# A routed transformer block on one core: the end of the router, the one-hot table products, the second layer's modulation and the W_down blocks rearranged

## The chip, the cores and the metric

The kernel runs on one core of a Trainium2 chip. The metric is device time in microseconds for one execution; a lower number is better. A core has a matrix engine (TensorE; the profile lists it as PE, and its weight loads as PEld), a vector engine (VectorE, DVE), an activation engine (ScalarE, ACT), a general engine (GpSimd, POOL) and a queue engine that issues transfers (SyncE, SP). They run side by side and wait for one another by semaphores. SBUF is the on-chip memory of 128 partitions, PSUM the memory that TensorE writes to, and everything larger lies in the chip's main memory.

## The reference, cut to what matters

Two transformer layers over 2048 tokens of width 512. Each layer is modulated by six vectors, made from a small vector c. Layer 0 has windowed attention and a mixture of 64 experts of which each token uses 8; layer 1 has attention and a gated feed-forward network with Hadamard transforms.

```python
mod = (_silu(L0_c) @ L0_wmod).reshape(1, 6, 1, -1)      # sa, ca, ga, sb, cb, gb
...
# router and experts of layer 0, x is (2048, 512)
probs = softmax(x @ gate_weight.T)                       # 64 experts
top_val, top_idx = lax.top_k(probs, 8)
top_val = top_val / top_val.sum(-1, keepdims=True)
mapping = ...                     # a secondary expert may be replaced by the most similar primary one
rerouted = mapping[top_idx]; rerouted[:, :4] = top_idx[:, :4]
order = argsort(rerouted.reshape(-1)); tok = order // 8
gate, up = split(ragged_dot(x[tok], gate_up_proj, group_sizes))
y = ragged_dot(silu(gate) * up, down_proj, group_sizes)
out = zeros_like(x).at[tok].add(y * w[:, None])
...
mod = (_silu(L1_c) @ L1_wmod).reshape(1, 6, 1, -1)       # layer 1's six vectors
...
# layer 1's feed-forward
x = fwht(x * SU_ug) / 64
x = silu((x @ W_gate.T) * s_gate) * ((x @ W_up.T) * s_up)
x = fwht(x * SU_dp) / 64
x = (x @ W_down.T) * s_dp
```

## The kernel before, in words

The 2048 tokens are 16 blocks of 128 (NT = 16, P = 128), kept in SBUF as x_sb. All matrix products are in 32-bit floats except the counting and one-hot ones, which are in 16-bit floats. A scheduler orders the instructions of each engine by their dependencies and the order of the program; `tc.issue_after` and the helper `in_turn` (L729) pin the order of some TensorE work to the order of the program.

**Attention of layer 0.** Half blocks are taken in turn; after every fourth block `route` (L432) sets two later steps. `logits` normalizes four blocks (xn_f), stores them in the main-memory table h_d, transposes them (nT_f) into hTr and multiplies by the gate weights (lg). `choose` takes the softmax, the best eight of each token (top), marks the chosen experts (sel) and transposes marks and shares (selT by st, pT by spT). While the attention runs, SP fills five sum tables in main memory (sums, NSUM = 5) with zeros; the source is the first slot of xring, a ring of NX = 12 slots of 128 x 576 numbers that later holds gathered token blocks.

**The router's end** (from L541). Counts of the choices (cnt), the map of replaced experts (map2), positions of each token in its expert's list (pf, and mT, the marks), the counts per expert (nq), a rank by size and its permutation (perm). `order` then gives SP the experts to fetch: `fetch_w` (L526) issues three transfers per expert, for the first four at once; the pool holds four experts' weights. Then the shares are brought into the order of ranks (pw, from mapT and mapr) and stored in h_d (L637); room, base, over, ot and the small products ops_ give the shift for lists longer than the room reserved for them, and jump and vT (L671 to L674) give each token's place in the table. vT is transposed (tv, L677) and copied to vm, and the eight largest entries per token (MAX8, L683) are split into a row, paf, and a column, tlf, of a table of 164 columns (ST = 164).

The table is written by one-hot products: for each block, hr marks the row (L692, then scaled by the token's number on ScalarE, L693) and hc the column (L695), each for all eight choices with the choice as the innermost index, and 128 products in all add up in tps:

```python
hr = rh.tile([P, P, TOPK], F16, tag="hr", name=f"hr_{i}")
V.tensor_tensor(hr, iota8[:, 0:P, :], bc(paf[:, i, :], 1, P), ALU.is_equal)
S.activation(hr, hr, AF.Copy, scale=con("tok1")[:, i : i + 1])
hc = rh.tile([P, ST, TOPK], F16, tag="hc", name=f"hc_{i}")
V.tensor_tensor(hc, iota8[:, 0:ST, :], bc(tlf[:, i, :], 1, ST), ALU.is_equal)
for k in range(TOPK):
    mm(tps, hr[:, :, k], hc[:, :, k], n == 0, n == NT * TOPK - 1)
```

From tps come hole and tidx (L701, L702), the table of token numbers from which GpSimd gathers. Small steps for lists that overflow follow (le, eps_, of, rps), and then `modulate` (L180) makes layer 1's six vectors: for each a 1 MB weight tile wm (two at a time), and either 16 products of one column (the four "col" vectors) or four products 512 wide (the two "gate" vectors). The matrix products all go through the helper on L129.

**The experts** (loop of L912). 64 runs of the table are taken in 32 pairs q. A run has up to ROOM[q] places (440 in the first pair, 184 in the last), in blocks of 128. `fetch_x` (L733) gathers a run's blocks from h_d into xring (L522), `x_T` transposes them (xp, L749) and modulates them (xT, L752 and L754), `gate_up` makes gu for both runs and gub for the two rests together, `down` makes y, scales it (yo, L804) and `add_rows` scatters it into the sum tables (L808). Pair 0's blocks are all transposed before its first product. Later pairs' transposes are spread between the products by `take`.

**Beside the experts**, VectorE and TensorE work on W_down: `gates` prepares small vectors, then `wd_step` (L848) takes eight blocks of 64 columns, each with four butterfly stages (L859, L860), two Hadamard products (wdh) and a store (L870) into wd_d. In the last quarter of the loop, `earlier` (L825) loads finished sum tables, in the memory of the W_down blocks, and adds them to x_sb.

**Layer 1** follows: attention, then the feed-forward loop that reads W_down back from wd_d as wd and multiplies four blocks by it (`down1`, L1264).

## Time and profile before

| | |
|---|---|
| time, median of 3 runs | 2269.71 us (2265.64 to 2273.39) |
| the profiled execution's own time | 2273.46 us |
| its span, first to last instruction | 2271.2 us |
| mean granted TensorE clock | 0.946 |
| busy share: PE, PEld, DVE, ACT, POOL | 93%, 51%, 37%, 21%, 25% |
| moved by DMA | 256.41 MB in 137350 packets, 52648 of them under 512 B |
| attention ends, cnt complete | about 331.6 us |
| tidx complete | 413.1 us |
| first expert product gu | 444.92 us |
| expert loop's last yo | about 1136 us |

How to read it: times inside the execution are microseconds from the start of the span. In a row of a group, the number after x is the count, then the total busy time and the mean in ns, and then the idle time in front of it with what ended it. A 32-bit matrix product shows as two records. The records of matrix products overlap, so the distance between two starts, not the length of one, is what a product costs in a row of them. The granted clock is 1.00 at full speed and 0.50 at half.

### The profile page before, as it was taken

Reading aid. Unit: us, or ns where it says so; the run is one execution under the profiler, and the core shown is the slowest. Engines: PE = TensorE matmul, PEld = TensorE weight load, DVE = VectorE, ACT = ScalarE, POOL = GpSimd, SP = SyncE. Lnnn points to the kernel's source line nnn. Section 1 sums busy time; section 2 is a strip of 40 time slices with the busy share of each in tenths; the row PEclk is TensorE's granted clock in tenths of the full one; section 3 lists DMA queues with packets and bytes.
Section 4 is the critical chain, followed back from the end, with each engine's and each line's share of the span. In section 5 each row is a group of like instructions: output and inputs, shape, how many; then the busy total and the mean of one; then the engine's idle time right before and its main releaser. Section 6 shows DMA issues by size and latency. Waiting matters only on the chain.

```text
span 2271.2 us, 27760 instructions
## 1 busy us (share of the span) xinstructions
PE 2103.9 (93%) x10584; PEld 1167.8 (51%) x10584; DVE 845.0 (37%) x2179; ACT 479.6 (21%) x1121; POOL 571.4 (25%) x448
## 2 busy tenths in 40 slices
PE   4899978899999999999809999998999999999999
PEld 3665555545555556666504555555444444444444
DVE  3236655154455433335547366765001011000101
ACT  0123423111111111111101166764010010010000
POOL 2300000366556666656424300110100010010000
PEclk9899975699999999999959989999999999999999
DMA  9800113569999989999862100003200000000000
GB/s 355 307 2 19 38 56 103 178 155 225 240 231 220 228 221 246 248 288 327 221 193 71 27 11 2 2 2 123 100 1 19 0 0 19 0 0 0 19 0 19
DMA packets 137350, 256.41 MB, mean 113 GB/s; under 512 B 52648, under 2 KB 55656, under 8 KB 134656
## 3 DMA queue, kind: packets, MB, share of 16 engines
q1 hardware_dynamic: 95136, 159.48, 21.1%
q0 software_dynamic: 36032, 77.30, 16.4%
q10 hardware_dynamic: 6048, 17.83, 2.1%
q8 instruction: 85, 1.39, 0.2%
q14 instruction: 49, 0.40, 0.1%
HBM read 180.56 MB, written 71.65 MB: 111 GB/s over the span
## 4 chain that ended last, share of the span: by engine, by line
PE 84%; DVE 6%; DMA 5%; ACT 3%; issue 1%; POOL 1%; ACTq 0%; POOLq 0%; DVEq 0%
PE y L129 19%; PE gu L129 10%; PE gate L129 10%; PE up L129 10%; PE gub L129 5%; PE s L129 4%; PE xp L749 4%; PE q L129 3%; PE po L129 3%; PE mod L129 3%; ACT pr L1123 2%; PE po_a L129 2%; PE pt L1141 2%; PE tps L129 2%; DMA wm<-in_L_wmod 2%; DMA sum<-yo,tidx 1%
## 5 line engine op out<-in xcount | busy, mean ns | idle before, releaser
L808 POOL DMA_INDIRECT sum<-yo,tidx x164 | 270.2, 1648 | 116.0 <-DMA sum<-yo,tidx 39.3
L522 POOL DMA_INDIRECT xring<-h_d,tidx x164 | 169.8, 1035 | 515.0 <-DVE tidx L702 331.4
L1280 DVE SCALAR_TENSOR_TENSOR act<-up,L_ws_up,sg 128x512 f32<-128x512 f32 x64 | 48.1, 751 | 587.0 <-PE up L129 587.0
L129 PE MATMUL gu<-xT,w 128*128 128x312 f32 (+26 forms) x1024 | 244.8, 397 | 5.4 <-DVE xT L754 5.4
L129 PE MATMUL gate<-xh,wug 128*128 128x512 f32 x512 | 232.3, 596 | 2.0 <-DMA wug<-in_L_Wug 2.0
L129 PE MATMUL up<-xh,wug 128*128 128x512 f32 x512 | 230.5, 592 | 0.0
L129 PE MATMUL y<-wd,act 128*128 128x512 f32 x512 | 229.5, 592 | 0.0
L129 PEld LDWEIGHTS gu<-xT,w 128*128 128x128 f32 x1024 | 191.4, 191 | 59.3 <-issue 16.7
L1278 ACT ACTIVATE sg<-gate,L_ws_gate 128x512 f32<-128x512 f32 x64 | 44.0, 687 | 570.1 <-PE gate L129 570.1
L129 PEld LDWEIGHTS gate<-xh,wug 128*128 128x128 f32 x512 | 97.4, 191 | 122.9 <-issue 120.7
L129 PEld LDWEIGHTS up<-xh,wug 128*128 128x128 f32 x512 | 97.3, 190 | 122.7 <-issue 122.5
L129 PEld LDWEIGHTS y<-wd,act 128*128 128x128 f32 x512 | 97.3, 190 | 122.5 <-issue 122.5
L129 PE MATMUL y<-w,hA 128*128 128x512 f32 (+22 forms) x328 | 148.8, 596 | 0.9 <-DVE yo L804 0.9
L804 DVE SCALAR_TENSOR_TENSOR yo<-y,wc,modr 128x512 f32<-128x512 f32 (+22 forms) x164 | 117.1, 746 | 78.7 <-PE y L129 61.5
L752 ACT ACTIVATE xT<-xp,modc,modc 128x312 f32<-128x312 f32 (+26 forms) x128 | 74.3, 580 | 314.0 <-PE xp L749 262.8
L259 POOL TENSOR_TENSOR xh<-hT 128x1024 f32<-128x1024 f32 x4 | 9.8, 2446 | 493.3 <-DVE xn_f L233 243.7
L129 PE MATMUL gub<-xT,w 128*64 128x312 f32 (+26 forms) x1024 | 125.4, 398 | 0.0
L1123 ACT ACTIVATE pr<-ng,nb 128x208 f32<-128x208 f32 (+1 forms) x256 | 115.5, 454 | 19.8 <-DVE nb L1113 19.8
L749 PEld LDWEIGHTS xp<-cst,xring 128*128 128x128 f32 x656 | 71.9, 141 | 68.0 <-issue 46.6
L749 PE MATMUL xp<-cst,xring 128*128 128x128 f32 x656 | 97.9, 281 | 1.9 <-DVE xT L754 1.2
L1113 DVE CUSTOM_DVE_ANT_0 ng<-s,cst 128x208 f32<-128x208 f32 (+1 forms) x256 | 87.2, 367 | 32.2 <-PE s L129 17.1
L770 DVE TENSOR_TENSOR hA<-hA,gu 128x312 f32<-128x312 f32 (+26 forms) x64 | 28.1, 440 | 186.3 <-PE xp L749 98.3
(313 smaller groups left out, 2613.5 us busy)
## 6 DMA issues: line engine op xcount, KB each, us to landing
w<-in_L_gu SPq DMA_DIRECT2D x64, 768.0 KB
sum<-xring SPq DMA_DIRECT2D x5, 4352.0 KB
w<-in_L_dn SPq DMA_DIRECT2D x64, 256.0 KB
wm<-in_L_wmod SPq DMA_DIRECT2D x9, 1024.0 KB
w<-in_L_dn SPq DMA_DIRECT2D x64, 128.0 KB
sa<-sum SPq DMA_DIRECT2D x32, 256.0 KB
h_d<-xn_f SPq DMA_DIRECT2D x16, 256.0 KB
wda<-in_L_Wdown SPq DMA_DIRECT2D x8, 512.0 KB
```

What stands on the lines that cost most here:

```text
L129: return TE.matmul(o, lhsT, rhs, start=start, stop=stop)
L522: return G.indirect_dma_start(out=dst, out_offset=None, in_=src[:, :], in_offset=bass.IndirectOffsetOnAxis(ap=idx, axis=0))
L749: st_["pe"] = TE.transpose(xp[:, b * P : (b + 1) * P], xg[:, c * P : (c + 1) * P], ident)
L752: S.activation(xT[:, c, 0:n], xp[:, 0:n], AF.Identity, bias=sh, scale=sc)
L770: V.tensor_tensor(o[:, 0:n], o[:, 0:n], ps[1][:, 0:n], ALU.mult)
L804: V.scalar_tensor_tensor(yo, ys[h], shares[h][rows, b : b + 1], m0[5][rows, :], ALU.mult, ALU.mult)
L808: G.indirect_dma_start(out=sums[k][:, :], out_offset=bass.IndirectOffsetOnAxis(ap=idx, axis=0), in_=yo, in_offset=None, compute_op=ALU.add,)
L1113: V.tensor_tensor_reduce(out=ng[:, :nk], in0=s[:, c2, :nk], in1=mask, scale=-SCALE, scalar=3e38, op0=ALU.add, op1=ALU.min, accum_out=nb,)
L1123: S.activation(prs[i, j][:, c, :nk], ng[:, :nk], AF.Exp, bias=nb, scale=-1.0, accum_out=totals[i][:, c, j : j + 1],)
L1141: TE.transpose(pt[0:n, c, :], pr[:, c, b * P : b * P + n], ident)
L1278: S.activation(sg, pg, AF.Silu, scale=wsg[:, f : f + 1])
L1280: V.scalar_tensor_tensor(acts[f], pu, wsu[:, f : f + 1], sg, ALU.mult, ALU.mult)
```

## The change

Seven edits.

- **Groups of routing.** The last four blocks are routed as two groups of two, at blocks 14 and 16; the first three groups stay four wide.
- **Order of the router's end.** ops_ and the jump and vT steps stand before the pw products. A helper, next_mm or next_T, pins these TensorE instructions to the order of the program.
- **One-hot columns.** hc has the choice as the outer index, so that each of its eight columns of 164 lies in one piece; each is made by a VectorE instruction of its own, which compares with a per-partition scalar (tl4). hr stays as it was.
- **Modulation of layer 1.** The weights are laid out as four steps of 128 inputs with all six vectors, 1.5 MB each, and loaded into the memory of xring: two steps early in the attention, the other two after their half of the memory has been read. Each step makes four products into 32 rows each and two into 128 rows, into the memory of mT and pf; the steps stand before the four groups of one-hot products. At the end the four column vectors are transposed.
- **Pair 0.** Its first run is transposed before gu, its second between gu's two halves; the fetch for pair 2 is issued after pair 0's gate_up.
- **W_down.** Four blocks of 128 columns instead of eight of 64; in main memory each block is contiguous, and the final matrix product reads wd in four pieces of 128.
- **Sum tables.** `earlier` uses one tile of [128, 4, 512] instead of two, alternately in the memory of the two W_down tiles.

```diff
+ROUTED = {4: 4, 8: 4, 12: 4, 14: 2, 16: 2}
...
-    wd_d = dram.tile([P, FC, D], F32, tag="wd_d", name="wd_d")
+    wd_d = dram.tile([KC, P, FC, P], F32, tag="wd_d", name="wd_d")
...
+    iota16 = rp.tile([P, NJ], F16, tag="iota16", name="iota16")
+    mod_w = {}
+    def mod_load(k):
+        w = xring.rearrange("p n d -> p (n d)")[:, 6 * D * (k % 2) : 6 * D * (k % 2 + 1)]
+        nc.sync.dma_start(out=w, in_=t["L1_wmod"][k].rearrange("p u d -> p (u d)"))
+        mod_w[k] = w.rearrange("p (u d) -> p u d", u=6)
...
             V.tensor_copy(iota8, bc(iota, 2, TOPK))
+            V.tensor_copy(iota16, iota)
+            mod_load(0)
+            mod_load(1)
...
-            def route(m, a):
-                g = m - 3
+            def route(g, n, a):
...
-                        if m % 4 == 3:
-                            route(m, a)
+                        if m + 1 in ROUTED:
+                            n = ROUTED[m + 1]
+                            route(m + 1 - n, n, a)
...
+    def in_turn():
+        return tc.issue_after(st_["pe"].ins) if "pe" in st_ else nullcontext()
+    def next_mm(*a):
+        with in_turn():
+            st_["pe"] = mm(*a)
+    def next_T(*a):
+        with in_turn():
+            st_["pe"] = TE.transpose(*a)
...
-            mm(ops_[:, 0:1], con("upto")[0:E, :], ot[0:E, :])
-            mm(ops_[:, 1:2], ones[0:E, :], ot[0:E, :])
+            next_mm(ops_[:, 0:1], con("upto")[0:E, :], ot[0:E, :])
+            next_mm(ops_[:, 1:2], ones[0:E, :], ot[0:E, :])
...
+                vTs.append(vT)
+            pw = rw.tile([P, NT, E], F32, tag="pw", name="pw")
...
+                    next_mm(pws[b][:, a, :], pT[r, a, :], mapr[r, :])
...
+            mods = [p_b.tile([P, 2, D], F32, tag=g, name=f"mod_{g}") for g in ("mT", "pf")]
+            cs1 = csil[:, 1, :]
+            csb = rw.tile([P, KC, P], F32, tag="csb", name="csb_1")
+            S.copy(csb, bc(cs1, 2, P))
+            def mod_step(k):
+                w = mod_w[k]
+                for u in range(4):
+                    next_mm(mods[0][32 * u : 32 * u + 32, 0, :], csb[:, k, 0:32], w[:, u, :], k == 0, k == KC - 1)
+                for u in range(2):
+                    next_mm(mods[1][:, u, :], csb[:, k, :], w[:, 4 + u, :], k == 0, k == KC - 1)
+                if k + 2 < KC:
+                    mod_load(k + 2)
+            mod_step(0)
             n = 0
             for b in range(2):
                 for h in range(2):
...
+                    tl4 = rh.tile([P, 4, TOPK], F32, tag="tl4", name=f"tl4_{i0}", bufs=2)
+                    V.tensor_copy(tl4, t8b[:, i4])
...
-                        hc = rh.tile([P, ST, TOPK], F16, tag="hc", name=f"hc_{i}")
-                        V.tensor_tensor(hc, iota8[:, 0:ST, :], bc(tlf[:, i, :], 1, ST), ALU.is_equal)
+                        hc = rh.tile([P, TOPK, ST], F16, tag="hc", name=f"hc_{i}")
                         for k in range(TOPK):
-                            mm(tps, hr[:, :, k], hc[:, :, k], n == 0, n == NT * TOPK - 1)
+                            V.tensor_scalar(hc[:, k, :], iota16[:, 0:ST], tl4[:, i - i0, k : k + 1], None, ALU.is_equal)
+                        for k in range(TOPK):
+                            next_mm(tps, hr[:, :, k], hc[:, k, :], n == 0, n == NT * TOPK - 1)
                             n += 1
+                    if 2 * b + h < 3:
+                        mod_step(2 * b + h + 1)
...
-            m1 = modulate(1, want, modp, rw, p_q, "q")
+            mrow = rw.tile([P, D], F32, tag="mrow", name="mrow")
+            S.copy(mrow, mods[0][:, 0, :])
+            for u, n in enumerate((2, 5)):
+                m1[n] = modp.tile([P, D], F32, tag=f"mod1{n}", name=f"modr_1_{n}")
+                S.copy(m1[n], mods[1][:, u, :])
+            mcol = mods[0][:, 1, :].rearrange("p (c q) -> p c q", c=KC)
+            for c in range(KC):
+                next_T(mcol[:, c, :], mrow[:, c * P : (c + 1) * P], ident)
...
-            a = h1.tile([P, 2, D], F32, tag="wda", name=f"sa_{i}", bufs=2)
-            b = h1.tile([P, D], F32, tag="wdb", name=f"sb_{i}", bufs=2)
+            a = h1.tile([P, 4, D], F32, tag=("wda", "wdb")[i % 2], name=f"sa_{i}")
...
-            a = h1.tile([P, FC, 64], F32, tag="wda", name=f"wda_{cb}", bufs=2)
-            b = h1.tile([P, FC, 64], F32, tag="wdb", name=f"wdb_{cb}", bufs=2)
-            nc.sync.dma_start(out=a, in_=t["L1_Wdown"][:, :, cols])
+        def wd_load(cb):
+            a = h1.tile([P, FC, P], F32, tag="wda", name=f"wda_{cb}")
+            nc.sync.dma_start(out=a, in_=t["L1_Wdown"][cb])
+            return a
...
-            nc.sync.dma_start(out=wd_d[:, :, cols], in_=dst)
+            nc.sync.dma_start(out=wd_d[cb], in_=dst)
...
-        take(turn(0), 2 * KC)
-        shares(0)
+        opening = turn(0)
+        take(opening, KC)
+        with tc.issue_after(st_["xv"].ins):
+            shares(0)
...
+                    lambda: take(opening, KC),
                 )
+            if q == 0:
+                fetch(2)
...
-                    mm(pos[a], act[:, a * P : (a + 1) * P], wd[:, f, :], f == 0, f == FC - 1)
+                    o = pos[a].rearrange("p (m d) -> p m d", m=KC)
+                    mm(o, act[:, a * P : (a + 1) * P], wd[:, :, f, :], f == 0, f == FC - 1)
```

## The prediction

> **What bounds the kernel now.** I read the page first (busy shares, slices, the chain that ended last), then the chain in order of time around the router's end, then busy time by stage, then single instructions there. The page puts most of the chain on TensorE matmuls, and two slices of its clock row, around 341 to 454 us, stand at 5 and 6 tenths while their PE digits are 8.
>
> ```profile
> PE   4899978899999999999809999998999999999999
> PEclk9899975699999999999959989999999999999999
> ```
>
> That is the router's end. Its chain, in order of time (start, length, what):
>
> ```profile
> 343.79 3.68 PE pw L129 x32
> 347.47 0.76 PE ops__2719 L129 x4
> ...
> 357.77 28.68 PE tps L129 x96
> 386.45 0.93 PE rps L129 x2
> 387.38 13.74 PE mod L129 x64
> 401.12 7.14 PE tps L129 x24
> 408.26 1.71 PE mod L129 x2
> 409.97 2.34 PE tps L129 x8
> 412.31 4.78 PE mod L129 x6
> 417.10 8.82 DMA wm<-in_L_wmod
> 425.93 0.14 issue
> 426.06 12.58 PE mod L129 x40
> ```
>
> See that 128 one-hot products (tps: 28.68 + 7.14 + 2.34 = 38.2 us), the modulation of layer 1 (mod) and a wait for its weights follow one another on one engine. The table index tidx ends at 413.1, the first expert matmul gu starts at 444.92. Busy time by stage (window, its length, then PE, PEld, DVE, ACT, POOL, granted clock, DMA share, GB/s):
>
> ```profile
> 357.00:386.00 29.00, 28.23 (x96) 13.89 (x96) 21.14 (x52) 15.42 (x14) 0.00 (x0) 0.50 0.16 41
> 386.00:401.00 15.00, 15.00 (x69) 14.19 (x68) 1.44 (x2) 1.20 (x2) 0.00 (x0) 0.50 0.20 71
> 417.00:426.00 9.00, 3.92 (x33) 3.83 (x31) 0.16 (x1) 0.59 (x1) 6.87 (x8) 0.67 0.93 313
> 478.00:530.00 52.00, 52.00 (x221) 27.09 (x220) 23.21 (x50) 7.36 (x13) 32.09 (x25) 1.00 0.93 230
> ```
>
> All of the router's end runs at half clock. In the expert stage (last row) PE is full, DMA nearly so.
>
> **The one-hot products.** In this stage's groups:
>
> ```profile
> L129 PE MATMUL tps<-hc,hr 128*128 128x164 f16 x96 | 28.7, 477 | 2.3 <-ACT hr L693 2.3
> L693 ACT ACTIVATE hr<-hr,cst 128x1024 f16<-128x1024 f16 x14 | 15.9, 1149 | 14.9 <-DVE hr L692 14.8
> L129 PEld LDWEIGHTS <-hr 128*128 128x128 f16 x96 | 13.9, 146 | 16.9 <-issue 9.0 <-ACT hr L693 2.9
> ```
>
> 28.68/96 = 0.299 us per product. The weight load is done after 0.146 and idles until the next product, so the stream of hc, taken at every eighth element, is the limit. Other f16 products here with contiguous operands (pf, 128 columns) are 0.107 us apart at the same clock, 0.83 ns per column; 164 columns would be 0.137. [...] By the row the weight load is 0.146, so I take 0.15 per product[...]. PE then needs 128 x 0.15 = 19.2 us.
>
> VectorE pays. Old hc: one instruction per token block, 0.74 us apart. New: eight per block, 128 in all, each 164 f16 elements against a pointer scalar, which the trace doesn't show. The nearest row has two pointers and f32:
>
> ```profile
> 312.72 1.91 DVE L233 TENSOR_SCALAR xn_f<-x_sb,mv_f,rs_f 128x512 f32<-128x512 f32 x4
> ```
>
> One lasts 0.54, so their spacing is (1.91-0.54)/3 = 0.457. The f32 scalar step with an immediate, same size (L210), is 0.33 apart: 0.06 more for each pointer. [...] I take 0.165. [...] Mine is 21.1, against 16 x 0.74 = 11.9 before.
>
> VectorE per block: 8 x 0.165 + hr 0.62 = 1.94; per group of four blocks four MAX8 at 0.13 and six small steps at 0.09 (one is new: tl4), 1.06. 16 x 1.94 + 4 x 1.06 = 35.3 us. ScalarE's hr scaling is 16 x 1.15 = 18.4, hidden. So VectorE becomes the bound; three buffers let it run ahead.
>
> **Modulation.** Before: 128 column products of one column and 8 row products; each shows as two records, 0.216 us a record for the columns, 0.85 for the rows: 37 us in all, plus 5.1 idle for wm. Now four steps, each four products into 32 rows of mT and two into 128, all 512 wide: two records of 0.85 a product at this clock. [...] The layer-1 attention has such products:
>
> ```profile
> 1502.46 0.64 PE L129 MATMUL o<-pts,va 128*32 128x256 f32 x8
> 1502.92 0.62 PE L129 MATMUL o<-pts,v 80*32 80x256 f32 x8
> ```
>
> Eight records take 0.46 us; in series, at full clock and 256 columns, each would be about 0.22 and the eight 1.8: four run at once. So a step is 2 x 0.85 + 4 x 0.85 = 5.1 us, four make 20.4 (in series 10.2 and 41). PE's total is 19.2 + 20.4 = 39.6, but step 0 lies before the first product, beside VectorE's first blocks (5 us), so PE needs some 34.5 where VectorE needs 35.3. They nearly tie; I add 1.2 for steps that hold a block back: 36.5. The last product, hole and tidx take 1.5. From vm (353.6) to tidx (413.1) it was 59.5; it becomes 38: **-21.5**.
>
> The weight loads: two 1.5 MB loads move from SP's queue at 330 to 421 us to the attention stage. They overwrite xring, the source of the zero fills, so SP waits until these have been read (their last issue is at 82.5, SP's queue is dry after 100.8). Behind them stand six small loads for later and the h_d stores, the first at 186: free. The other two stand behind the 12 expert weight loads and the h_d store of pw, each waiting for a step; step 2 wants its data some 19 us after step 0[...]. Behind them is only wda. The removed wm at 417 to 426 takes its stall with it.
>
> **Before that stage.** ops_ waited behind pw on PE (347.47); its input ot is there at 343.4. It now goes first, and pw and its store lie beside the two vT chains on VectorE: **-4**. The last four blocks are routed 2 + 2: 16 instead of 32 lg records behind the last projection (0.22 each: 3.5 us) and two blocks' choosing less (1.6 + about 1), but oT and po of block 14 now stand behind the logits of 12 and 13 on PE, with their evacuations and one more table load (1.28): about +5. Net **-1** (0 to -3).
>
> **After it.** Gathers start 0.9 us after tidx and are 1.25 apart; block run 0 needs four: 0.9 + 3 x 1.25 + 0.95 + about 2 to land = 7.6 us, formerly hidden under mod. Then transposes and evacuation of run 0 alone, 3.4: gu starts 11 us after tidx instead of 31.8: **-21**. The tail of the modulation (mrow, four transposes, four copies, about 3 us) lies under the gathers. Given back: run 1's transposes stand between gu's halves, 3 us, and PE comes cold out of the wait, so the first half (6 us at full clock) loses about 2.5: **+5.5**.
>
> **W_down.** Same butterflies (64 at 0.6 become 32 at about 1.1), same 16 products, other sizes; 16 MB-halves in 256-byte pieces (2048 each; SP spends 7.8 us on one wda) become eight 1 MB moves in whole rows. PE is full beside them and waited for DMA only near 1093, when they are over: 0. Bounds: -6 (less DMA pressure) to +4 (longer VectorE steps ahead of yo and xT, on which PE waits for p_y). The sums' load tile and fetch order: 0, as buffers, not order, release them. In the last stage the moving operand comes in four pieces of 128; s<-kbd has four pieces of 64 and no loss: 0.
>
> **Sum.** -1 - 4 - 21.5 - 21 + 5.5 = -42. The profiled execution is 2273.46 us (span 2271.2 and 2.3 around it), 3.75 above the median of the three runs, 2269.71. On it: 2231.5; on the median: **2228 us**. The expert stage and all behind it shift as a whole.
>
> **Rivals.**
> *The stage keeps PE's pace* (0.20). The strided weights hold products at 0.299[...]: 128 x 0.149 = +19 on PE beside the modulation[...], or the narrow products run in series, +20 on PE. For: hr's stride stays. Against: the load's 0.146, the row of o. About 2246.
> *More comes* (0.16). Modulation hides fully (-1), the clock rises in the router's end, W_down's larger pieces ease the late waits (-6): about 2219.
> *The gain is swallowed* (0.03): the scatter chain at 1093 to 1157, or DMA at 0.93, paces the experts, so that an earlier start buys waiting. Against: PE shows no wait from 445 to 1093. About 2267.
> *Slower* (0.03). One mechanism: fixed cost per VectorE piece. The gain is gone at 0.165 + 42/128 = 0.49 us a piece; at 0.55 it is 7 us slower, 2277. The two-pointer step of three times the size takes 0.457, hence small.
> Forecast as summed: 0.58.
>
> **Numbers.** A difference below 0.3% (6.8 us) can't be told from none here. Forecast, first and second rival make faster 0.94. The forecast's own range is 2221 to 2235; two tenths left out gives 2214 to 2249.
>
> **What would show it.** tps products about 0.15 us apart or waiting for DVE hc; hc pieces 0.165 apart; tidx near 387; gu near 398; no wm wait; POOL and DMA, not PE mod, in the chain ahead of the first xp; expert stage about 690 us as before. Wrong, if products stay at 0.3, if gu starts after 415, or if the stage from gu to the last yo grows.

## The result, and the profile after

The changed kernel takes 2244.66 us (median of four runs, 2239.90 to 2248.46) against 2271.12 us beside it: ratio 0.9886, 95% interval 0.9859 to 0.9913. It was run once more later, beside other kernels: 2251.28 us against 2270.59, ratio 0.9915 (0.9894 to 0.9936). The forecast was 2228 with a range of 2214 to 2249: the first median lies inside it, the later one 2 us above its top. The change gave some 19 to 26 us where 42 were expected. The profiled execution took 2248.46 us, its span is 2246.6 us (before: 2271.2), and its mean granted clock 0.957 (0.946).

The router's end lies in slices 6 to 8 of the page. The clock row has 8, 7 and 8 there (7, 5 and 6 before), and the matrix engine is no fuller:

```profile
PE   4899977999999999998838999998999999999999
PEclk9899987899999999999969989999999999999999
```

Read the other dent, too: slices 19 to 21 (1011 to 1179 us) hold PE at 8, 8 and 3, where before slice 19 was full. That is the last quarter of the expert stage and its end, and part of the gain is lost there.

The end of the router in the chain of waits (start, length, what):

```profile
354.03 1.38 DVE hc L748 x8
...
366.97 1.22 DVE hc L748 x7
...
368.21 1.31 PE tps L131 x8
369.52 1.87 PE mod_mT L131 x8
...
373.31 0.74 PE tps L131 x10
...
386.15 1.31 PE tps L131 x8
...
390.14 1.18 POOL xring L548
...
401.41 0.73 PE gu L131
```

The chain now runs over VectorE's hc and hr, with the products and one modulation step in between. Ten tps records take 0.74 us. tidx starts at 388.8 (412.8 before), gu at 401.41 (444.92), and before the first xp the gather stands where mod and the wait for wm stood. The groups of the stage:

```profile
L748 DVE TENSOR_SCALAR hc<-iota,tl 128x164 f16<-128x164 f16 x128 | 23.7, 256 | 0.0
L131 PE MATMUL tps<-hc,hr 128*128 128x164 f16 x128 | 13.2, 252 | 9.8 <-DVE hc L748 8.8 <-ACT hr L745 1.0
L131 PEld LDWEIGHTS <-hr 128*128 128x128 f16 x128 | 11.1, 148 | 13.7 <-ACT hr L745 12.5 <-issue 1.1
```

VectorE does not stand at all ahead of hc (0.0), PE waits for it nine times: VectorE is the bound, as forecast. Eight pieces take 1.38 us in the chain (the row at 354.03), 0.172 each. By stage (columns as in the tables before: length, busy PE, PEld, DVE, ACT, POOL, granted clock, DMA share, GB/s), the router's end and the experts after, and then the experts before:

```profile
350.00:387.00 37.00, 27.21 (x179) 15.23 (x179) 36.19 (x184) 20.60 (x22) 0.00 (x0) 0.87 0.59 210
424.00:1094.00 670.00, 652.71 (x3191) 384.48 (x3188) 290.63 (x619) 104.95 (x210) 409.80 (x300) 0.99 0.90 236
```

```profile
463.00:1093.00 630.00, 629.14 (x3102) 371.93 (x3098) 286.80 (x638) 102.44 (x204) 390.41 (x290) 1.00 0.94 244
```

VectorE is busy 36.2 of 37 us in the router's end. In the experts PE stood for 0.9 us of 630 before and stands for 17.3 of 670 now: 3.8 of them between pairs 3 and 15, 12.0 between pairs 25 and 29. That is where to look.

A ledger makes this readable. In every profile I took the start of the second group of gate-up products (gub) of each pair from the timeline of PE; the *lead* is how much earlier it starts than in the kernel before. Of the changed kernel: 38.9 us at pair 0, 41.0 at pair 3, 32.5 at pair 15, the same 32.5 still at pair 25, 13.8 at pair 29, 18.0 at pair 31, 28.3 where layer 1 begins (in the chain of waits its first load of sin, which follows the last scatters, starts at 1158.63 and 1130.29), 24.6 at the end of the span. The router did nearly what was summed; two stretches of the experts, pairs 4 to 15 and 26 to 29, gave it back. These are the stretches in which VectorE works on W_down and in which it adds the sum tables. (The 2.1 us that the lead gains up to pair 3 are work put off: PE's first W_down products stood in pair 1 before and stand in pair 3 now.)

### The profile page after: what moved, and what is told of

It is laid out like the page before. It is cut to its first block, busy times and chain, and to the rows that moved or that the text cites. A ratio compares the mean times of both kernels' runs of the same rounds, so it can differ in the third digit from the quotient of the medians.

```text
span 2246.6 us, 27640 instructions
## 1 busy us (share of the span) xinstructions
PE 2068.8 (92%) x10492; PEld 1136.5 (51%) x10492; DVE 854.1 (38%) x2280; ACT 483.8 (22%) x1130; POOL 573.7 (26%) x448
## 3 DMA queue, kind: packets, MB, share of 16 engines
q0 software_dynamic: 36032, 77.30, 16.7%
q8 instruction: 84, 1.38, 0.3%
## 4 chain that ended last, share of the span: by engine, by line
PE 76%; DMA 9%; DVE 8%; ACT 3%; issue 2%; POOL 1%; SPq 1%; ACTq 0%; POOLq 0%; DVEq 0%
PE y L131 17%; PE up L131 9%; PE gate L131 9%; PE gu L131 9%; PE gub L131 4%; PE s L131 4%; PE q L131 3%; DMA sa<-sum 3%; PE xp L814 3%; PE po L131 3%; ACT pr L1206 2%; PE pt L1224 2%; PE po_a L131 2%; DMA wda<-in_L_Wdown 2%; PE v L131 1%
## 5 line engine op out<-in xcount | busy, mean ns | idle before, releaser
L131 PEld LDWEIGHTS gu<-xT,w 128*128 128x128 f32 x1024 | 191.9, 192 | 55.1 <-issue 18.2
L131 PE MATMUL y<-w,hA 128*128 128x512 f32 (+22 forms) x328 | 152.1, 602 | 18.6 <-DVE yo L871 18.5
L837 DVE TENSOR_TENSOR hA<-hA,gu 128x312 f32<-128x312 f32 (+26 forms) x64 | 28.2, 440 | 192.2 <-PE xp L814 109.7
L1196 DVE CUSTOM_DVE_ANT_0 ng<-s,cst 128x208 f32<-128x208 f32 (+1 forms) x256 | 87.1, 366 | 31.7 <-PE s L131 16.7
## 6 DMA issues: line engine op xcount, KB each, us to landing
xring<-in_L_wmod SPq DMA_DIRECT2D x4, 1536.0 KB, 10.5
wda<-in_L_Wdown SPq DMA_DIRECT2D x4, 1024.0 KB, 14.2
```

Of the source, the lines that this page charges most:

```text
L131: return TE.matmul(o, lhsT, rhs, start=start, stop=stop)
L837: V.tensor_tensor(o[:, 0:n], o[:, 0:n], ps[1][:, 0:n], ALU.mult)
L1196: V.tensor_tensor_reduce(out=ng[:, :nk], in0=s[:, c2, :nk], in1=mask, scale=-SCALE, scalar=3e38, op0=ALU.add, op1=ALU.min, accum_out=nb,)
```

## Experiments

The columns of the ledger for all profiles: start of the first operation that waits for cnt; start of tidx; lead at pairs 0, 16 and 29; and the time from gub of pair 25 to layer 1's first load of sin, which holds all that the end of the expert stage costs.

| kernel | after cnt | tidx | lead 0 | lead 16 | lead 29 | pair 25 to layer 1 | median us | ratio (95%) |
|---|---|---|---|---|---|---|---|---|
| before | 331.7 | 412.8 | 0 | 0 | 0 | 138.1 | 2271.12 | |
| changed | 331.8 | 388.8 | 38.9 | 32.5 | 13.8 | 142.3 | 2244.66 | 0.9886 (0.9859 to 0.9913) |
| after_again (the same) | 336.5 | 392.9 | 29.0 | 22.5 | 5.9 | 138.7 | 2251.28 | 0.9915 (0.9894 to 0.9936) |
| router_only | 337.6 | 394.0 | 28.0 | 27.9 | 28.0 | 136.8 | 2240.95 | 0.9857 (0.9831 to 0.9883) |
| tail_only | 330.9 | 412.0 | 0.9 | -4.9 | -23.4 | 147.4 | 2284.22 | 1.0052 (1.0032 to 1.0072) |
| wd_ahead | 336.7 | 393.1 | 30.7 | 29.0 | 11.9 | 141.1 | 2249.01 | 0.9905 (0.9882 to 0.9929) |
| own_tiles | 336.7 | 393.1 | 30.9 | 24.4 | 24.5 | 137.2 | 2246.87 | 0.9889 (0.9870 to 0.9908) |
| routed_four | 330.0 | 387.1 | 36.9 | 31.3 | 14.8 | 143.4 | 2250.55 | 0.9908 (0.9890 to 0.9926) |
| router_four | 330.9 | 387.9 | 36.0 | 36.0 | 34.9 | 137.1 | 2234.82 | 0.9845 (0.9824 to 0.9865) |
| router_four_again (the same) | 331.6 | 388.7 | 34.7 | 34.7 | 34.1 | 136.0 | 2239.15 | 0.9867 (0.9847 to 0.9887) |
| strided | 336.8 | 412.3 | 11.3 | 6.0 | -11.4 | 142.7 | 2269.35 | 0.9995 (0.9985 to 1.0005) |
| columns_only | 330.4 | 400.5 | 12.4 | 12.4 | 11.1 | 139.4 | 2259.31 | 0.9948 (0.9930 to 0.9966) |
| both_first | 330.3 | 387.4 | 38.4 | 38.4 | 37.3 | 137.1 | 2235.80 | 0.9843 (0.9823 to 0.9862) |
| both_split | 331.7 | 388.5 | 37.7 | 37.7 | 37.3 | 139.1 | 2234.85 | 0.9842 (0.9829 to 0.9856) |

Executions of one kernel lie up to 18 us apart (the kernel before: 2264.30 to 2282.17 in one series), so single terms of 5 us are read from the leads inside a trace, and only sums of them from the times.

**router_only: the change without its two edits in the experts.** W_down in eight blocks of 64 columns and the sum tables in two tiles, both as in the kernel before.

```diff
-            a = h1.tile([P, 4, D], F32, tag=("wda", "wdb")[i % 2], name=f"sa_{i}")
-            parts = [a[:, k, :] for k in range(3)]
+            a = h1.tile([P, 2, D], F32, tag="wda", name=f"sa_{i}", bufs=2)
+            b = h1.tile([P, D], F32, tag="wdb", name=f"sb_{i}", bufs=2)
+            parts = [a[:, 0, :], a[:, 1, :], b]
...
-            for cb in range(KC):
-                yield from wd_step(cb, a)
+            for cb in range(8):
+                yield from wd_step(cb)
```

> The changed kernel with W_down and the loads of the partial sums as they were before: only the Router part and the opening of the first pair are new. Theory A (the Router part brings about 40 us and the two edits in the expert stage give 15 of it back): a lead of 39 to 41 us that holds from pair 1 to pair 29 and a time of 2230 to 2234. Rival C (an earlier start of the experts is swallowed by the end of the stage whatever W_down does, by the scatter chain or the DMA engines): 2240 to 2245.

The lead does not move at all: 28.0, 27.9, 28.0. So the losses belong to these two edits and not to an earlier start; the third rival of the prediction, that the end of the stage swallows the gain, falls. The size was a miss: the lead is 28, not 39 to 41, and the time, 2240.95, lies where rival C had it, though not for C's reason. This profile begins its experts later than the changed kernel's first profile; the last experiments come back to that.

**tail_only: the two edits alone, in the kernel before.**

```diff
-    wd_d = dram.tile([P, FC, D], F32, tag="wd_d", name="wd_d")
+    wd_d = dram.tile([KC, P, FC, P], F32, tag="wd_d", name="wd_d")
...
-            a = h1.tile([P, 2, D], F32, tag="wda", name=f"sa_{i}", bufs=2)
-            b = h1.tile([P, D], F32, tag="wdb", name=f"sb_{i}", bufs=2)
+            a = h1.tile([P, 4, D], F32, tag=("wda", "wdb")[i % 2], name=f"sa_{i}")
...
+        def wd_load(cb):
+            a = h1.tile([P, FC, P], F32, tag="wda", name=f"wda_{cb}")
+            nc.sync.dma_start(out=a, in_=t["L1_Wdown"][cb])
```

> The kernel before with W_down in four blocks of columns and with the partial sums loaded into one tile, nothing else of the change. Theory A: 8 us lost in pairs 4 to 15, 14 us in pairs 26 to 29, of which the shorter scatter chain gives some 8 back: 2283 to 2288 against about 2271. Rival C (these edits cost nothing by themselves and only the earlier start made them late): 2269 to 2273.

As theory A has it: 2284.22 us, ratio 1.0052 with an interval above 1. By the ledger 5.8 us go between pairs 0 and 16 and 18.5 more by pair 29. Half of these 18.5 come back at the end of the stage: from pair 25 to layer 1 it takes 147.4 us against 138.1, only 9.3 more. The two edits cost this with the router of before, too.

**own_tiles: only the sum tables' tiles.**

```diff
-            a = h1.tile([P, 4, D], F32, tag=("wda", "wdb")[i % 2], name=f"sa_{i}")
-            parts = [a[:, k, :] for k in range(3)]
+            a = h1.tile([P, 2, D], F32, tag=("wda", "wdb")[i % 2], name=f"sa_{i}")
+            b = h1.tile([P, D], F32, tag="sb", name=f"sb_{i}", bufs=2)
+            parts = [a[:, 0, :], a[:, 1, :], b]
```

> The changed kernel with the early partial sums in two tiles per block again: two parts in the buffer that W_down leaves, the third in a small tile of its own. Theory A (the single tile of three parts is released only by the third addition, so all but two loads of a pair stand behind the next weight fetches): the lead over the kernel before at the second gate-up group of pairs 26 to 29 stays what it is at pair 25, and the lead at the end of the profiled execution is about that of pair 25 and not 8 us less; the median falls by 6 to 9 us, to 2236 to 2239. Rival B (the additions are late because of the scatters or the load of the DMA engines): the lead still falls by 10 us or more between pairs 25 and 29, the time stays at 2243 to 2247.

SP's queue in the changed kernel, during pair 24 (its gub starts at 970.85):

```profile
980.18 0.81 SPq L897 DMA_DIRECT2D sa<-sum  x2
981.23 0.34 SPq L560 DMA_DIRECT2D w<-in_L_dn  x1
...
984.70 4.37 SPq L897 DMA_DIRECT2D sa<-sum  x4
```

and with two tiles, at the same place (gub of pair 24 at 978.91):

```profile
985.30 2.55 SPq L898 DMA_DIRECT2D sa<-sum  x4
988.25 0.92 SPq L898 DMA_DIRECT2D sb<-sum  x2
```

Six loads feed the next pair's additions. With two tiles all six are in the queue 6.4 to 10.3 us after gub. With one tile the first two come at 9.3 us and the other four at 13.9 to 18.2, behind five weight transfers (one is shown): the tile is free only after the third addition of its block, which is the last step of its kind on VectorE. What that does on the chain of waits of the changed kernel:

```profile
985.96 9.56 DMA sa<-sum
...
997.36 0.76 DVE yo L871
...
998.16 2.88 PE y L131 x6
```

VectorE stands at an addition until the load lands, yo stands behind it on the same engine, and PE's y waits for yo: 20.6 us at eight y from 960 to 1110 us. The additions' waits in the changed kernel (what ended them, us, times):

```profile
  DMA sa<-sum: 17.2, 6
```

With two tiles no addition waits for a load, and the lead keeps its 24.4 us from pair 16 to 29 (24.5). So theory A's mechanism is shown and rival B falls, though the time, 2246.87, lies in B's range and not at 2236 to 2239. One reason is the start: this profile's lead at pair 0 is 30.9, not 38.9. From there theory A's other sign held: the lead at the end of the span is 25.6, about that of pair 25. The last column has the other reason: of the 16 to 19 us that the lead falls by pair 29 with one tile, not all is net. From the last y of the experts to layer 1's load of sin the six profiles with one tile take 12.0 to 14.1 us, the eight with two take 21.7 to 25.5. The kernel before ends its experts with scatters that wait for each other: seven start after the last yo (1134.44), and four waits for sum<-yo,tidx stand in the chain (5.16, 4.32, 4.92 and 3.71 us). With the stretched pairs of the changed kernel three start after the last yo (1116.41); the others have run by then. From pair 25 to layer 1 the six take 138.7 to 147.4 us, mean 142.6, and the eight take 136.0 to 139.4, mean 137.6. The net price is about 5 us, and times alone can't resolve it.

Two whole new tiles for the sums (own_sums) can't be had: with them the pool needs 34.75 KB of each partition, and 30.84 are free. So own_tiles leaves the first two parts in the memory of the W_down tiles.

**wd_ahead: a second buffer for the loaded W_down block.**

```diff
-            a = h1.tile([P, FC, P], F32, tag="wda", name=f"wda_{cb}")
+            a = h1.tile([P, FC, P], F32, tag="wda", name=f"wda_{cb}", bufs=2)
...
-            a = wd_load(0)
+            loads = [wd_load(0), wd_load(1)]
...
-                yield from wd_step(cb, a)
-                if cb + 1 < KC:
-                    a = wd_load(cb + 1)
+                yield from wd_step(cb, loads[cb])
+                if cb + 2 < KC:
+                    loads.append(wd_load(cb + 2))
```

> The changed kernel with a second buffer for the loaded block of W_down, so that each block is loaded a whole block ahead; the partial sums keep their single tile. Theory A1 (of the 8.5 us that pairs 4 to 15 lose, most is VectorE standing before the first addition of a block until its load lands): 5 to 6 us come back, 2238 to 2240. Rival A2 (the pieces of 1.22 us in place of 0.69 us on VectorE delay the yo behind them): at most 2 us come back, 2243 to 2246.

The sums' tile goes with it, as two buffers in the memory of wda instead of one in wda and one in wdb. In the changed kernel's chain the load of a block is on the path three times; the first (start, length, what):

```profile
523.16 15.19 DMA wda<-in_L_Wdown
...
540.76 0.75 DVE yo L871
...
541.55 2.19 PE y L131 x6
```

With one buffer the load can only be issued when the block before is done with it, and its 1 MB takes 14.2 us in the median from issue to landing (9.2 to 15.2) beside the weight fetches. The tile's waits in the changed kernel (idle time of the engine ahead of the tile's instructions: what ended it, us, times):

```profile
  DMA wda<-in_L_Wdown: 5.0, 3
  DVE wdb L936: 3.5, 6
```

With two buffers the first of these lines is gone and the second is the same, and between pairs 0 and 16 the lead falls by 1.7 us, not 6.4. So 4.7 of the 6.4 us are the load, and about 1.7 us remain for the longer pieces (1.22 us each, 0.69 before) or for what else the new schedule moves; these two were not told apart. The time, 2249.01, lies above both expected ranges and does not show it: this profile starts with a lead of 30.7.

**strided: the one-hot columns as before, all else changed.**

```diff
-                        hc = rh.tile([P, TOPK, ST], F16, tag="hc", name=f"hc_{i}")
-                        for k in range(TOPK):
-                            V.tensor_scalar(hc[:, k, :], iota16[:, 0:ST], tl4[:, i - i0, k : k + 1], None, ALU.is_equal)
+                        hc = rh.tile([P, ST, TOPK], F16, tag="hc", name=f"hc_{i}")
+                        V.tensor_tensor(hc, iota8[:, 0:ST, :], bc(tlf[:, i, :], 1, ST), ALU.is_equal)
                         for k in range(TOPK):
-                            next_mm(tps, hr[:, :, k], hc[:, k, :], n == 0, n == NT * TOPK - 1)
+                            next_mm(tps, hr[:, :, k], hc[:, :, k], n == 0, n == NT * TOPK - 1)
```

> The changed kernel with the one-hot columns as before: one tile of columns by ranks, written by one instruction, each product reading every eighth element. Theory S (the product with every eighth element is what paced the stage, about 0.30 us each at half clock as in the kernel before, and the modulation steps add their 2.9 to 5.1 us each on top): from the first vm copy to tidx 57 to 62 us instead of 39.5, and 2262 to 2268. Rival M (taking the modulation off the end and keeping VectorE ahead is what shortened the stage, the form of the columns matters little): 40 to 46 us, 2244 to 2251.

Its chain of waits is PE from end to end:

```profile
359.99 9.48 PE tps L131 x32
369.47 1.86 PE mod_mT L131 x8
```

9.48/32 = 0.296 us a product, as in the kernel before, and from the first vm copy to tidx 58.4 us. The whole remaining change is worth a lead of 11.3 at pair 0, the experts take that back, and the kernel is level with the one before (0.9995, interval 0.9985 to 1.0005; 1.4 us above the top of what was expected). The read of every eighth element is what paced the stage: in columns_only, where each column lies in one piece, the last 32 products take 4.43 us (395.41 to the next start at 399.84), 0.138 each, at a clock of 0.50. The 1.86 us of mod_mT here are those of half clock (1.87 in the changed kernel).

**columns_only: the contiguous columns alone, in the kernel before.**

```diff
-                        hc = rh.tile([P, ST, TOPK], F16, tag="hc", name=f"hc_{i}")
-                        V.tensor_tensor(hc, iota8[:, 0:ST, :], bc(tlf[:, i, :], 1, ST), ALU.is_equal)
+                        hc = rh.tile([P, TOPK, ST], F16, tag="hc", name=f"hc_{i}")
                         for k in range(TOPK):
-                            mm(tps, hr[:, :, k], hc[:, :, k], n == 0, n == NT * TOPK - 1)
+                            V.tensor_scalar(hc[:, k, :], iota16[:, 0:ST], tl4[:, i - i0, k : k + 1], None, ALU.is_equal)
+                        for k in range(TOPK):
+                            mm(tps, hr[:, :, k], hc[:, k, :], n == 0, n == NT * TOPK - 1)
```

> The kernel before with the one-hot columns each in one piece and nothing else of the change; the modulation stays behind the one-hot stage. Theory D (with short products the stage is set by VectorE at about 39.5 us instead of 59.5, and the modulation's 31.8 us stay on the path after it): first vm copy to tidx 38 to 41 us, 2249 to 2253. Rival E (the loads of W_mod or the half clock keep the stage near 50 us): 2260 to 2266.

Neither theory: 2259.31 us, and 48.6 us from vm to tidx. PE's timeline shows what both forgot:

```profile
381.74 13.81 PE L129 MATMUL mod<-csil,wm 128*128 128x1 f32 x64
395.41 4.63 PE L129 MATMUL tps<-hc,hr 128*128 128x164 f16 x32
```

Twelve blocks run at VectorE's pace, 1.97 us each within a group. Then 64 records of modulation (32 products), which nothing pins behind, come ahead of the last 32 one-hot products, and tidx waits 14 us for them. In the stage itself, from vm to tidx, everything but the columns saves 1 us of 59.5 (strided), the columns alone 11, both together 20. Short products leave PE idle beside VectorE (in columns_only 10.9 us ahead of the 128 products, for hc 7.0 and for hr 3.9), the modulation steps fill such idle time, and the pinned order (next_mm) keeps them from delaying tidx. At pair 0, where the earlier end of the modulation counts too, the gains nearly add: columns alone bring a lead of 12.4, and on top of the rest 16.7 (28.0 in router_only against 11.3 in strided, both with the operation after cnt at 337).

**Where the experts start: routed_four, router_four and the repeats.** The remaining question was why the lead at pair 0 is 28 in some profiles and 39 in another. routed_four is the changed kernel, router_four the kernel of router_only, each with one line more:

```diff
-ROUTED = {4: 4, 8: 4, 12: 4, 14: 2, 16: 2}
+ROUTED = {4: 4, 8: 4, 12: 4, 16: 4}
```

> The changed kernel with four blocks in every routing group, as before. Theory R (the two-block groups leave TensorE gaps near 300 us in which its granted clock falls, which in two profiles of three put the first operation after cnt at 337 us instead of 332): with groups of four it is at 331 to 333 us in every profile and the median is 2 to 5 us lower, 2240 to 2243. Rival P (as predicted, two-block groups save about 1 us, and the 337 us are chance): 2244 to 2247.

> The changed kernel with W_down, the loads of the partial sums and the routing groups all as before; what is left of the change is the order of the Router's end, the one-hot pieces, the modulation steps and the opening of the first pair. Theory A with theory R: no loss in pairs 4 to 29 and the first operation after cnt at 332 us, so a lead of 33 to 40 us that holds to the end, 2232 to 2238. Rival: the lead of 28 us of the kernel with W_down and the sums as before was what the Router part is worth, 2240 to 2244.

> The changed kernel, unaltered, run beside the others. If W_down and the loads of the partial sums cost what the traces show (8 us in pairs 4 to 15, 4 to 9 us net after pair 25), it lies 10 to 15 us above the kernel with groups of four and W_down and sums as before: 2245 to 2250. If its first measurement of 2244.7 was the rule and the start of the experts differs by kernel, it lies within 8 us of that kernel.

> The kernel with groups of four and with W_down and the partial sums as before, for the comparison on one chip: 2233 to 2237 by either theory of the experts.

With groups of four in both, W_down and sums as before are 15.7 us faster (2234.82 against 2250.55). Of the repeats, router_four_again is 12.1 us faster than after_again, where 10 to 15 were expected; this pair differs in the routing too, and each came out 1 to 2 us above its expected range. That is of the size of the 6.4 + 5 from the ledgers and of the 12 us (ratio 1.0052) of tail_only. Theory R is half borne out: the first operation after cnt stands at 330 to 332 in every profile with groups of four, and at 336.5 or later in five of the six with two-block groups up to here, but routed_four is no faster than the changed kernel (2250.55 against 2244.66 and 2251.28).

**both_first and both_split.** both_first is router_four with the transposes of both first runs ahead of the products, both_split the same with two-block groups again.

```diff
         opening = turn(0)
-        take(opening, KC)
+        take(opening, 2 * KC)
```

> The same kernel with the transposes of both runs of the first pair ahead of its products, as before the change. Theory O (putting the second run's transposes between the gate-up halves costs a pause of 4.8 us on TensorE, because both VectorE and ScalarE stand for something the trace calls remote until 411 us, and the pause would lie beside products if the transposes came first): the first gate-up starts 3 to 5 us later, its second group of products starts 3 to 5 us earlier, 2230 to 2233. Rival (the pause comes with these instructions wherever they stand): the second group starts at the same time or later, 2235 to 2239.

> The fastest kernel so far (groups of four, W_down and partial sums as before, both runs' transposes ahead of the first products) with one edit: the last four blocks in two routing groups of two, as in the change. Theory R (the two-block groups open TensorE gaps near 300 us, its clock falls earlier, and what waits for cnt is 5 us late): first operation after cnt at 336 to 338 us instead of 330, the lead at the first pair 5 to 6 us smaller, 2239 to 2242. Rival P (no cost; the profiles that showed 337 us were chance): 330 to 333 us, 2233 to 2237.

In eight of the nine profiles with the new opening, router_four_again among them, PE stands for 4.1 to 5.4 us between the two halves of pair 0's gate-up, because VectorE and ScalarE stand at the same time. First PE, then VectorE:

```profile
413.66 1.97 PE L814 MATMUL xp<-cst,xring 128*128 128x128 f32 x8 [5.00 <-DVE xT L819]
```

```profile
412.34 0.61 DVE L837 TENSOR_TENSOR hA<-hA,gu 128x440 f32<-128x440 f32 x1 [9.93 <-remote]
```

The view calls the releaser remote when it can't name one. The signals in the packed trace say more: both engines wait for PE. After PE's records of the last gu and of the five transposes that signal, which end at 407.78 to 408.66, PE's next six signals stand at 412.25 to 412.45; in the changed kernel's first profile, the one without the pause, the six (409.43 to 410.30) follow the ends of their records by 0.01 to 0.02 us. PE's signals come late, most of them in a bunch, in all eight. What held them, or PE itself, stays open. With both transposes first there is no such wait in either profile; in both_first PE runs all 32 gate-up records from 404.80 on without a break:

```profile
404.80 13.54 PE L131 MATMUL gu<-xT,w 128*128 128x440 f32 x32
```

gu starts 17.4 us after the start of tidx, 5.4 later than in router_four_again, and gub nevertheless 2.4 us sooner (31.5 against 33.9 us after tidx). By the times, 2235.80 is within the noise of router_four's two medians and in the rival's range. Theory O is right on the trace, and its price was smaller than expected.

both_split came out where rival P had it, 331.7 after cnt and 2234.85 us: two-block groups need not cost anything, and they save nothing that shows here. What puts cnt at 337 is a clock that falls earlier. The windows of after_again and of both_split, which have the same instructions here:

```profile
305.00:310.00 5.00, 4.56 (x21) 4.13 (x20) 0.77 (x3) 0.75 (x2) 0.00 (x0) 0.50 0.01 2
```

```profile
305.00:310.00 5.00, 4.33 (x21) 2.66 (x21) 1.55 (x7) 2.18 (x3) 0.00 (x0) 1.00 0.00 0
```

At 0.50 the logits of blocks 12 and 13 and the projection behind them take some 4 us longer, and the rest of the router moves with them: up to 303 us the two profiles' instructions lie a steady 0.9 us apart, from 314 us on 4.8. The operation after cnt was late in five of the seven profiles with two-block groups, each time with the clock at 0.50 to 0.53 from 305 to 310 us, and in none of the seven with groups of four. So theory R is not refuted: that two-block groups open the way to the early fall remains likely by these counts, and that it never happens with groups of four isn't shown. Nor is it shown that gaps of PE bring the clock down: from 300 to 305 us PE is busy for 3.33 us in after_again, where the clock falls, and for 3.10 in both_split, where it does not. A third possibility is untested: the two on-time profiles with two-block groups, the changed kernel's first and both_split, also hold the most records of transfers' signals (11927 and 12058; all others 9974 to 10304), so the recording itself may have a part in it.

both_split, both_first and router_four can't be told apart (2234.85, 2235.80, and 2234.82 with 2239.15 in its repeat). The first two are 35 to 37 us below the kernel before and 9 to 16 below the change.

## Why the prediction was right and wrong

- **Router's end before the stage, -1 and -4.** ops_ and the vT chain: 21.6 us from the first operation after cnt to the first vm copy before, 17.8 after, so -3.8. Routing: +0.1 in the first profile, against -1; up to 6 later in others, 4 of it by the clock.
- **The stage, -21.5.** From the first MAX8 to the end of tidx 59.5 us became 39.2, so -20.3. Its steps held: hc 0.172 us apart (0.165 taken, the author's estimate, which no row of before shows), VectorE the bound, the narrow modulation products four at once (eight records in 1.07 us at full clock, 1.87 at half; four wide records take 1.98 at full clock). The strided weights, which the first rival had holding products at 0.299, did not hold them: their load stayed at 0.148, and products came 0.074 us apart at full clock. On the side of the stream the stride does cost, as strided's 0.296 shows (0.138 in columns_only). The clock rose (0.87 from 350 to 387 us, against 0.50 from 357 to 386 before), which rival "more comes" had, and gave nothing, since VectorE, busy for 36.2 of these 37 us, set the pace. The four loads of modulation weights took 10.5 us in the median from issue to landing, and no product waited for them.
- **After it, -21.** tidx to gu took 12.3 us instead of 11: -19.5.
- **Given back, +5.5.** 4.6 in the first profile (17.2 us from gu to gub where it was 12.6 before; the first half of gu took 8.2 us and the second 6.1, so PE did come out of the wait at half clock, 0.50 from 385 to 405 us). 11.0 in after_again (23.6 us), 5.4 of it the pause that no row of before could show.
- **W_down, 0, with bounds of -6 and +4: failed.** It cost 6.4 us, more than the bound of +4. The working counted instructions and bytes, found both equal or better, and asked what PE waits for, not what VectorE waits for ahead of yo. Two half-size buffers had let the next load run during a block, and VectorE never waited for one; one full-size buffer starts it after the block, and the load, 14.2 us in the median, has not landed when the next block's first addition is due (three waits, 5.0 us). yo stands behind that addition. The bound had named longer VectorE steps ahead of yo; they are at most the 1.7 us that wd_ahead leaves.
- **The sums' load tile, 0, "as buffers, not order, release them": failed,** by its own rule. Buffers release them, and the edit changes the buffers: three parts in one tile are released by the third addition, two parts by the second, and the pair's loads are issued up to 18.2 us after gub instead of 10.3. 16 to 19 us were lost between pairs 25 and 29, about 5 net on average.
- **"The expert stage and all behind it shift as a whole": failed** with these two. One of the prediction's own signs of being wrong came true: the stage from gu to the last yo grew, from 691 us (444.92 to 1136.0) to 716 (401.41 to 1117.9). Layer 1 lost another 3.7 us in the first profile (lead 28.3 at its start, 24.6 at its end); in the others it lost up to 3.8 or gained up to 4.2, and no cause was found for that.

The sum for the first profile: 38.9 us at pair 0 (42 predicted), less 6.4, less 4.2 (142.3 against 138.1), less 3.7, is 24.6, the difference of the spans. That the range held the first median is luck: its top was set by other ways of losing 18 us, and the loss was not foreseen. The later median, 2251.28, lies outside.

Two readings in the working are off without changing a sum: the "128 column products" are 64 products in 128 records, and the router's end did not all run at half clock, as its own row at 417 shows (0.67).

## What to carry to other kernels

When an edit merges tiles or halves the number of buffers, list for each what releases it and behind which instructions that release and the next load stand: here, with equal bytes and no more instructions, W_down's edit cost 6.4 us of the lead by pair 16 and that of the sums another 16 to 19 by pair 29, about 5 net. On an engine that feeds the critical one, ask what stands behind a side task: VectorE waited 17.2 us for the loads of its additions, yo stood behind them, and PE's y waited 20.6 us for yo. Such loads had to land before their turn. And two edits that look separate, shorter products and modulation in between, can be worth more together than alone (1 and 11 us in the stage, 20 together), because one makes the idle time that the other fills.

## What was not expected of the hardware

The same instructions ran at 0.50 or 1.00 of the clock near 305 us in different profiles, which moved the router's end by 4 us. In the router's end the clock was 0.87 with PE busy 27.2 of 37 us in the changed kernel, 0.50 with PE busy 28.2 of 29 us in the kernel before (the row at 357 in the prediction), and 0.50 with PE busy 6.1, 6.2 and 5.7 of three 10 us windows in columns_only: the share of busy time that the profile counts does not tell the granted clock there. In pair 0 PE's signals reached VectorE and ScalarE some 3 to 5 us after the records of its products had ended, in eight profiles of nine; the ninth is one of the two with the fullest records.
